# Feed-forward stage of a two-layer graph network: DVE operands moved from SBUF into PSUM, and a third PSUM bank for the down products

## Chip, cores and metric

The kernel runs on one core of one Trainium2 chip. The metric is device time in microseconds (us) of one execution; lower is better. PE is the matrix engine, DVE the vector engine, ACT the scalar engine, POOL the engine that issues indirect DMAs here, SP the queue of plain DMAs.

## What is computed

There are 10,000 nodes with 512 features and 160,000 edges sorted by destination. Cut to what matters:

```python
h = maximum(layernorm(x), 0)                                 # layer 0
msg = (h @ rel_W[r] + rel_b[r])[src]                         # r: type of the edge, 4 types
agg = segment_sum(msg, dst) / maximum(deg, 1)
x1  = layer_norm(h + h @ self_W + self_b + agg) * ln1_w + ln1_b
f   = gelu(x1 @ W1 + b1) @ W2 + b2                           # 512 -> 1024 -> 512
x   = x + layer_norm(x1 + f) * ln2_w + ln2_b
h   = maximum(layernorm(x), 0)                               # layer 1: two rounds of
h   = relu(h @ W_self + mean_over_edges(h) @ W_neigh + b)    # this line, then
out = x + h                                                  # the residual
```

## The kernel before

All is fp32, in blocks of 128 nodes: a first block of 16 nodes (called "full" in the code, the remainder of 10,000), then blocks 0 to 77. The program has four stages, told apart in the trace by the lines that run: preparation (the products per edge type, L724, and lists of edges, to about 1230 us of the span), the **feed-forward stage** (about 1230 to 3030 us, the first `with` in `aligned`), and two aggregation stages that end at 6251.8 us. The change touches the feed-forward stage alone.

**One round of the feed-forward stage** (the loop at L1107) handles one block. Its steps stand in each engine's queue in the order of the code; no scheduler reorders them, and every engine works its queue in order.

- `gather` (L790) makes POOL issue the indirect DMAs of the *next* block: 5 `orow` tiles and 11 `row` tiles of 128x512, and on every 4th (16th) block one (two) `srow` tiles. They land in a ring of 28 SBUF tiles (`rows`), so POOL may run ahead until a slot is still in use.
- `hots` (L811) makes DVE compare the constant `lane` (0 to 127 along the row) with the local indices `loc` and so write one-hot matrices for the next block (L820, 128x896).
- `second` (L1035) takes the finished down products `po`: DVE adds the residual `rest` to each (L1042, result in SBUF) and takes statistics (L1013, L1014).
- `add` (L854) makes DVE add the 11 `row` tiles into the block's PSUM bank `pa` (L858), after `sums` (L831) let PE put the one-hot products of the `orow` and `srow` tiles there (L847). L1126 scales the sum and adds the node's own value `xs`, and statistics follow.
- `products` (L1086) is the PE work of the round, before the next block's sums: a part of a group's feed-forward, and `turn` (L958), the transposes of the block of the round before (L963).
- `finish` (L1017) makes the scale factors: square root on ACT (L1020), then two small DVE steps (L1022, L1023). `scaled` (L1047) applies the norms: ACT subtracts and scales (L1028), DVE multiplies by the weight and adds (L1067 and L1068 for the first norm, L1072 and L1073 for the second).

A group is four blocks, and its feed-forward is spread over the four rounds after the one of its successor's first block. By the block number b of the round they are called here **A** (b mod 4 = 1: half of the up products, L975, with Gelu on ACT, L977), **B** (b mod 4 = 2: the other half), **C** (b mod 4 = 3: down products d0 and d1, L986) and **D** (b mod 4 = 0: d2 and d3). The first D is in the round of block 8, the last in that of block 76: 18 of them. In C and D the order on PE is: first product, transposes, second product, sums of the next block. In the first rounds PE also has 24 products of a kind put off from the preparation (`residuals`, L921, `LATE` says how many a round; each ends in a DVE addition, L928).

**PSUM** has eight banks of 128x512 fp32 here: `psA` 2 (`pa`), `psT2` 2 (transposes), `psH` 2 (up products), `psO` 2 (down products and `residuals`). A bank is taken again when the last reader of what it held is done.

Of the kernel before, what the change touches and what calls it, by code (L numbers as in the profile page):

```python
# [8 lines left out]
F32 = mybir.dt.float32  # L9
# [4 lines left out]
OP = mybir.AluOpType  # L14
# [7 lines left out]
def kernel(  # L22
# [739 lines left out]
    def aligned(ctxa):  # L762
# [27 lines left out]
        def gather(b, table, pool, split):  # L790

            def rows(n, idx, name=None, bufs=None):
                t = pool.tile([P, D], F32, name=name, bufs=bufs) if name else row_tile()
                nc.gpsimd.indirect_dma_start(  # L794
                    out=t[:n], out_offset=None, in_=table,
                    in_offset=bass.IndirectOffsetOnAxis(ap=idx, axis=0))
# [12 lines left out]
            return others, [rows(P, row[:, b, t:t + 1]) for t in range(own(b))]  # L809

        def hots(b, pool, scalar=False):  # L811
            n = OT + NL if b < full else OT_LAST
            hot = pool.tile([P, OT + NL, P], F32, name="hot", bufs=2)
            if scalar:
                for t in range(n):
                    nc.scalar.activation(hot[:, t, :], lane, AF.Abs, bias=loc[:, b, t:t + 1],  # L816
                                         scale=-1.0)
                nc.scalar.activation(hot[:, :n], hot[:, :n], AF.Relu, bias=ones[:, :1], scale=-1.0)
                return hot
            nc.vector.tensor_tensor(hot[:, :n].bitcast(F32R),  # L820
                                    lane[:, None, :].to_broadcast([P, n, P]),
                                    loc[:, b, :n].unsqueeze(2).to_broadcast([P, n, P]),
                                    op=OP.is_equal)
            return hot
# [3 lines left out]
            for _ in range(n):  # L828
                nc.tensor.matmul(p, ident, w, start=True, stop=True)  # L829

        def sums(b, others, hot, idle=None):  # L831

            r, n = height(b), len(others)
            pa = psA.tile([P, D], F32, name="pa")
# [15 lines left out]
        def begin(b, hot, table, pool, idle=None, split=False):  # L850
            others, mine = gather(b, table, pool, split)
            return sums(b, others, hot, idle), mine

        def add(b, pa, mine):  # L854

# [5 lines left out]
        with ExitStack() as s:  # L861
# [1 line left out]
            wp = s.enter_context(tc.tile_pool(name="wp2", bufs=1))  # L863
            gp = s.enter_context(tc.tile_pool(name="gp", bufs=1))
            sp = s.enter_context(tc.tile_pool(name="sp", bufs=3))
            psT = s.enter_context(tc.tile_pool(name="psT2", bufs=2, space=PSUM))
            psH = s.enter_context(tc.tile_pool(name="psH", bufs=2, space=PSUM))
            psO = s.enter_context(tc.tile_pool(name="psO", bufs=2, space=PSUM))
            w1s = wp.tile([P, KC, F], F32, name="w1s")
            w2s = wp.tile([P, FC, D], F32, name="w2s")  # L870
            b1s = wp.tile([P, FC], F32, name="b1s")
# [60 lines left out]
            fetch(LATE[0])  # L932
            for b in blocks[:2]:
                load(b)
            first_hot = hots(blocks[0], gp)
# [63 lines left out]
            class Scales:  # L999
# [27 lines left out]
                def apply(self, out, v, c, r, func):  # L1027
                    nc.scalar.activation(out, v, func, bias=self.rs[:r, 1, c:c + 1],  # L1028
                                         scale=self.rs[:r, 0, c:c + 1])

            rests = {}
            fed, third = [], []
            now = Scales()

            def second():  # L1035

                nonlocal fed
                got = []
                for b, po in fed:
                    r = height(b)  # L1040
                    v = rests.pop(b)
                    nc.vector.tensor_tensor(v[:r], po[:r], v[:r], op=OP.add)  # L1042
                    got.append((b, v, now.stats(v[:r], r)))
                fed = []
                return got

            def scaled(got, first):  # L1047

                nonlocal third, now
                if first:  # L1050
                    b, c = first
                    r, v = height(b), nodes[b]
                    now.apply(v[:r], v[:r], c, r, AF.Identity)
                if third:
                    h1, at = pair(h1_d, third[0][0], len(third), "h1", 2)
                    for k, (b, c) in enumerate(third):
                        now.apply(h1[:, k, :], xrs.pop(b), c, height(b), AF.Relu)
                    nc.sync.dma_start(at, h1)
                third = []
                for b, v, c in got:  # L1060
                    r = height(b)
                    now.apply(v[:r], v[:r], c, r, AF.Identity)
                if first:
                    b, c = first
                    r, v = height(b), nodes[b]
                    rests[b] = gp.tile([P, D], F32, name="rest", bufs=11)
                    nc.vector.tensor_tensor(rests[b][:r], v[:r], ln1w[:r], op=OP.mult)  # L1067
                    nc.vector.tensor_tensor(rests[b][:r], rests[b][:r], lnb2[:r], op=OP.add)  # L1068
                now = Scales()
                for b, v, c in got:  # L1070
                    r = height(b)
                    nc.vector.tensor_tensor(v[:r], v[:r], ln2w[:r], op=OP.mult)  # L1072
                    nc.vector.tensor_tensor(xrs[b], xrs[b], v[:r], op=OP.add)  # L1073
                    third.append((b, now.stats(xrs[b], r)))
                if got:
                    b, n = got[0][0], len(got)
                    nc.sync.dma_start(rows_of(xn_d, (b, n, height(b))), xrs.pop((b, n)))
# [5 lines left out]
            held = begin(blocks[0], first_hot, table, gp, split=True)  # L1083
            nc.vector.tensor_tensor(lnb2, lnb2, b2s, op=OP.add)

            def products(work, turned):  # L1086
# [20 lines left out]
            for bs in plan:  # L1107
                for b in bs:
                    r = height(b)
                    if b == bs[0]:  # L1110
                        before, grp = grp, Group(bs)
                    if i + 2 < len(blocks):
                        load(blocks[i + 2])
                    if i + 1 < len(blocks):
                        hot = hots(blocks[i + 1], gp)
                    ready = []
                    if i + 2 < len(LATE):
                        fetch(LATE[i + 2])
# [7 lines left out]
                    nc.vector.scalar_tensor_tensor(v[:r], pa[:r], rdeg[:r, b:b + 1], v[:r],  # L1126
                                                   op0=OP.mult, op1=OP.add)
                    first = (b, now.stats(v[:r], r))
                    part = products(queue.pop(0) if queue else [], turning)
                    next(part)  # L1130
                    now.finish()
                    scaled(got, first)
                    next(part, None)
                    if i + 1 < len(blocks):
                        held = begin(blocks[i + 1], hot, table, gp, split=True)
# [411 lines left out]
```

## Time and profile before

| | us |
|---|---|
| runs: median of 3 (lowest to highest) | 6250.86 (6247.69 to 6256.69) |
| the profiled execution: its own time | 6253.56 |
| the profiled execution: span of its instructions | 6251.8 |
| feed-forward stage: window 1400 to 2900, PE busy | 1427.8 of 1500 |
| the same, POOL busy | 1148.7 of 1500 |
| the same, DVE busy | 1127.8 of 1500 |

The page groups instructions by line, engine, operands and shape, with busy time and the mean of one in ns. The timeline gives start and length of single instructions (a row with "xN" merges N in a row), with the idle time before them in brackets and what ended it. A window view sums the busy time of each engine between two times, with the clock that PE was granted (1.00 is full speed). The page counts no instruction that only issues or waits, so POOL's rows are the issues of its gathers. In PE's rows a 128x512 product over 128 rows is two matmul instructions.

### The profile page before, as it was taken

Reading aid. Unit: us, or ns where it says so; the run is one execution under the profiler, and the core shown is the slowest. Engines: PE = TensorE matmul, PEld = TensorE weight load, DVE = VectorE, ACT = ScalarE, POOL = GpSimd, SP = SyncE. Lnnn points to the kernel's source line nnn. Section 1 sums busy time; section 2 is a strip of 40 time slices with the busy share of each in tenths; the row PEclk is TensorE's granted clock in tenths of the full one; section 3 lists DMA queues with packets and bytes.
Section 4 is the critical chain, followed back from the end, with each engine's and each line's share of the span. In section 5 each row is a group of like instructions: output and inputs, shape, how many; then the busy total and the mean of one; then the engine's idle time right before and its main releaser. Section 6 shows DMA issues by size and latency. Waiting matters only on the chain.

```text
span 6251.8 us, 54551 instructions
## 1 busy us (share of the span) xinstructions
PE 5699.4 (91%) x14875; PEld 2517.3 (40%) x14875; DVE 3597.1 (58%) x7253; ACT 1858.2 (30%) x3672; POOL 3762.9 (60%) x3927
## 2 busy tenths in 40 slices
PE   9999999989999999999788888888879888888888
PEld 3444444444444444444333333333333333333333
DVE  8768889557777777776344444344334444444444
ACT  1016565013333333333322222222222222222221
POOL 0001110057777777775477777777767777777776
PEclk9999999989999999999899999999999999999999
DMA  4333344387887878886577777777778788878877
GB/s 162 114 117 118 122 136 154 132 275 243 255 256 242 256 246 252 256 257 196 187 234 237 237 234 237 237 234 237 237 232 251 249 247 251 250 246 251 250 246 217
DMA packets 503498, 1373.74 MB, mean 220 GB/s; under 512 B 82206, under 2 KB 82206, under 8 KB 503054
## 3 DMA queue, kind: packets, MB, share of 16 engines
q0 software_dynamic: 308768, 1008.91, 54.0%
q1 hardware_dynamic: 193886, 360.20, 15.9%
q8 instruction: 120, 1.97, 0.1%
q14 instruction: 196, 1.61, 0.1%
q10 hardware_dynamic: 528, 1.05, 0.1%
HBM read 1156.54 MB, written 213.30 MB: 219 GB/s over the span
## 4 chain that ended last, share of the span: by engine, by line
DMA 40%; PE 39%; DVE 8%; issue 7%; POOL 5%; ACT 1%; POOLq 0%; SPq 0%; DVEq 0%; ACTq 0%
DMA rows<-h_d,row 19%; PE pm L724 15%; DMA rows<-h_d,orow 14%; PE pa L847 6%; POOL rows L794 5%; PE ph L975 5%; PE po L986 4%; DVE pa L858 4%; DMA rows<-hall_d,row 4%; PE pm L664 3%; PE po L1218 1%; PE po L926 1%; DVE st L1013 1%; PE pT L172 1%; DMA tail<-h_d,srow 1%
## 5 line engine op out<-in xcount | busy, mean ns | idle before, releaser
L858 DVE TENSOR_TENSOR pa<-pa,rows 128x512 f32<-128x512 f32 x2574 | 1799.3, 699 | 2061.3 <-PE pa L847 1241.3
L794 POOL DMA_INDIRECT rows<-h_d,row x1716 | 1622.2, 945 | 522.7 <-issue 291.2
L847 PE MATMUL pa<-rows,hot 128*128 128x512 f32 (+1 forms) x2358 | 1247.7, 644 | 371.4 <-DMA rows<-h_d,orow 314.2
L794 POOL DMA_INDIRECT rows<-hall_d,row x858 | 868.1, 1012 | 273.6 <-issue 109.0
L794 POOL DMA_INDIRECT rows<-h_d,orow x786 | 743.1, 945 | 354.4 <-DMA h_d<-h 99.0
L847 PEld LDWEIGHTS pa<-rows,hot 128*128 128x128 f32 (+1 forms) x2358 | 407.1, 194 | 1151.9 <-DMA rows<-h_d,orow 829.0
L794 POOL DMA_INDIRECT rows<-hall_d,orow x393 | 378.2, 962 | 346.0 <-DVE hg L666 202.2
L986 PE MATMUL po<-w2s,hid 128*128 128x512 f32 (+1 forms) x1264 | 566.6, 602 | 17.2 <-DVE rest L1042 14.0
L1218 PE MATMUL po<-wss,hTb 128*128 128x512 f32 (+1 forms) x1264 | 579.7, 602 | 0.0
L1189 PE MATMUL po<-wns,mTb 128*128 128x512 f32 (+1 forms) x1264 | 573.5, 597 | 1.4 <-ACT mTb L173 1.4
L975 PE MATMUL ph<-x1T,w1s 128*128 128x512 f32 (+2 forms) x1344 | 558.7, 568 | 4.8 <-ACT hid L977 4.8
L173 ACT COPY mTb<-pT 128x512 f32<-128x512 f32 (+1 forms) x158 | 91.8, 581 | 1233.5 <-PE pT L172 1233.5
L1214 ACT ACTIVATE mb<-pa,rdeg 128x512 f32<-128x512 f32 (+1 forms) x158 | 108.5, 687 | 1130.0 <-DVE pa L858 1127.8
L829 PE MATMUL pa<-wss,ident 128*128 128x512 f32 x936 | 427.5, 593 | 0.0
L508 POOL DMA_INDIRECT win<-rec_d,at x79 | 76.0, 962 | 545.9 <-PE pe L533 364.8
L1189 PEld LDWEIGHTS po<-wns,mTb 128*128 128x128 f32 (+1 forms) x1264 | 240.2, 190 | 308.4 <-issue 272.4
L975 PEld LDWEIGHTS ph<-x1T,w1s 128*128 128x128 f32 x1344 | 249.4, 192 | 282.0 <-issue 273.4
L986 PEld LDWEIGHTS po<-w2s,hid 128*128 128x128 f32 (+1 forms) x1264 | 237.6, 191 | 308.2 <-issue 283.4
L847 PE MATMUL pa<-tail,hot 128*128 128x512 f32 x624 | 308.1, 611 | 50.6 <-DMA tail<-h_d,srow 47.1
L816 ACT ACTIVATE hot<-lane,loc 128x128 f32<-128x128 f32 x1098 | 337.7, 391 | 0.0
L1218 PEld LDWEIGHTS po<-wss,hTb 128*128 128x128 f32 (+1 forms) x1264 | 233.5, 195 | 235.3 <-issue 234.9
L724 PE MATMUL pm<-wrel,hT 128*128 128x512 f32 x624 | 296.5, 597 | 0.0
(289 smaller groups left out, 6224.5 us busy)
## 6 DMA issues: line engine op xcount, KB each, us to landing
hall_d<-p SPq DMA_DIRECT2D x156, 256.0 KB, 2.5
hall_d<-u SPq DMA_DIRECT2D x156, 256.0 KB, 2.4
hb<-h_d SPq DMA_DIRECT2D x156, 256.0 KB, 4.3
rows<-h_d,row POOLq DMA_INDIRECT x1716, 3.8
xg<-in_x_dram SPq DMA_DIRECT2D x39, 512.0 KB, 3.6
xr_d<-xg SPq DMA_DIRECT2D x39, 512.0 KB, 3.0
xs<-xs_d SPq DMA_DIRECT2D x39, 512.0 KB, 7.6
h_d<-h SPq DMA_DIRECT2D x39, 512.0 KB, 4.5
```

Of the source, the lines that this page charges most:

```text
L664: nc.tensor.matmul(pm[:r], rows[3][:, c, k, :r], wself[:, k, :], start=(k == 0), stop=(k == KC - 1))
L724: nc.tensor.matmul(pm, a[:, k, :], w[:, k, :], start=(k == 0), stop=(k == KH - 1))
L794: nc.gpsimd.indirect_dma_start(out=t[:n], out_offset=None, in_=table, in_offset=bass.IndirectOffsetOnAxis(ap=idx, axis=0))
L816: nc.scalar.activation(hot[:, t, :], lane, AF.Abs, bias=loc[:, b, t:t + 1], scale=-1.0)
L829: nc.tensor.matmul(p, ident, w, start=True, stop=True)
L847: nc.tensor.matmul(pa[:r], h, v, start=(i == 0), stop=(i == len(work) - 1))
L858: nc.vector.tensor_tensor(pa[:r], pa[:r], t[:r], op=OP.add)
L975: nc.tensor.matmul(ph[:, :n], w1s[:, k, f * P:(f + 1) * P], self.xT[:, k, :n], start=(k == 0), stop=(k == KC - 1))
L986: nc.tensor.matmul(po[:r], self.hid[:, f, c * r:(c + 1) * r], w2s[:, f, :], start=(f == 0), stop=(f == FC - 1))
L1189: nc.tensor.matmul(po[:r], mT[:, k, :r], wns[:, k, :], start=False, stop=(k == KC - 1))
L1214: nc.scalar.activation(m[:r], pa[:r], AF.Copy, scale=rdeg[:r, b:b + 1])
L1218: nc.tensor.matmul(po[:r], hT[:, k, :r], wss[:, k, :], start=(k == 0), stop=False)
```

## The change

- `hots` no longer reads `lane` in SBUF: ACT copies it into the first 128 columns of the PSUM bank that the next block's sums will use (the bank is now taken there, `bank()`), and DVE compares from PSUM. `sums` gets the bank handed in.
- L1126's result stays in `pa` (PSUM); statistics and ACT's normalisation read it there, and ACT writes the normalised rows to `xs` in SBUF for the transposes. `second` leaves its sum in `po`.
- `affine` takes the place of L1067/L1068 and, with ACT's L1028 on `rest`, of L1072/L1073: two DVE steps, (v - mean) * weight in place in PSUM, then * scale + addend (`lnb2`, or the residual `xr`) into SBUF.
- In `scaled` the second norm's steps (`got`) now come before the first norm's (`first`).
- `psO` has three banks, `psT2` one.

```diff
-        def hots(b, pool, scalar=False):
+        def hots(b, pool, scalar=False, pa=None):
...
+            nc.scalar.copy(pa[:, :P], lane)
             nc.vector.tensor_tensor(hot[:, :n].bitcast(F32R),
-                                    lane[:, None, :].to_broadcast([P, n, P]),
+                                    pa[:, None, :P].to_broadcast([P, n, P]),
                                     loc[:, b, :n].unsqueeze(2).to_broadcast([P, n, P]),
                                     op=OP.is_equal)
...
-            psT = s.enter_context(tc.tile_pool(name="psT2", bufs=2, space=PSUM))
+            psT = s.enter_context(tc.tile_pool(name="psT2", bufs=1, space=PSUM))
             psH = s.enter_context(tc.tile_pool(name="psH", bufs=2, space=PSUM))
-            psO = s.enter_context(tc.tile_pool(name="psO", bufs=2, space=PSUM))
+            psO = s.enter_context(tc.tile_pool(name="psO", bufs=3, space=PSUM))
...
+                def affine(self, out, v, c, r, w, to):
+
+                    nc.vector.scalar_tensor_tensor(v, v, self.mv[:r, c, 0:1], w[:r],
+                                                   op0=OP.subtract, op1=OP.mult)
+                    nc.vector.scalar_tensor_tensor(out, v, self.rs[:r, 0, c:c + 1], to,
+                                                   op0=OP.mult, op1=OP.add)
...
-                    v = rests.pop(b)
-                    nc.vector.tensor_tensor(v[:r], po[:r], v[:r], op=OP.add)
-                    got.append((b, v, now.stats(v[:r], r)))
+                    nc.vector.tensor_tensor(po[:r], po[:r], rests.pop(b)[:r], op=OP.add)
+                    got.append((b, po, now.stats(po[:r], r)))
...
-                    now.apply(v[:r], v[:r], c, r, AF.Identity)
+                    now.apply(nodes[b][:r], pa[:r], c, r, AF.Identity)
...
-                for b, v, c in got:
+                last, now = now, Scales()
+                for b, po, c in got:
                     r = height(b)
-                    now.apply(v[:r], v[:r], c, r, AF.Identity)
+                    last.affine(xrs[b], po[:r], c, r, ln2w, xrs[b])
+                    third.append((b, now.stats(xrs[b], r)))
                 if first:
...
-                    nc.vector.tensor_tensor(rests[b][:r], v[:r], ln1w[:r], op=OP.mult)
-                    nc.vector.tensor_tensor(rests[b][:r], rests[b][:r], lnb2[:r], op=OP.add)
-                now = Scales()
-                for b, v, c in got:
-                    r = height(b)
-                    nc.vector.tensor_tensor(v[:r], v[:r], ln2w[:r], op=OP.mult)
-                    nc.vector.tensor_tensor(xrs[b], xrs[b], v[:r], op=OP.add)
-                    third.append((b, now.stats(xrs[b], r)))
+                    last.affine(rests[b][:r], pa[:r], c, r, ln1w, lnb2[:r])
...
                     if i + 1 < len(blocks):
-                        hot = hots(blocks[i + 1], gp)
+                        next_bank = bank()
+                        hot = hots(blocks[i + 1], gp, pa=next_bank)
...
-                    nc.vector.scalar_tensor_tensor(v[:r], pa[:r], rdeg[:r, b:b + 1], v[:r],
+                    nc.vector.scalar_tensor_tensor(pa[:r], pa[:r], rdeg[:r, b:b + 1], v[:r],
                                                    op0=OP.mult, op1=OP.add)
-                    first = (b, now.stats(v[:r], r))
+                    first = (b, now.stats(pa[:r], r), pa)
```

More of the change, by code (lines that the diff above doesn't have):

```diff
@@ L829, in keep_busy, with bank, sums @@
                 nc.tensor.matmul(p, ident, w, start=True, stop=True)
-        def sums(b, others, hot, idle=None):
+        def bank():
+            return psA.tile([P, D], F32, name="pa")
+        def sums(b, others, hot, idle=None, pa=None):
             r, n = height(b), len(others)
-            pa = psA.tile([P, D], F32, name="pa")
+            pa = pa or bank()
             if idle:
@@ L848, in sums, with begin @@
             return pa
-        def begin(b, hot, table, pool, idle=None, split=False):
-            others, mine = gather(b, table, pool, split)
-            return sums(b, others, hot, idle), mine
+        def begin(b, hot, table, pool, idle=None, pa=None):
+            others, mine = gather(b, table, pool, pa is not None)
+            return sums(b, others, hot, idle, pa), mine
         def add(b, pa, mine):
@@ L934, in aligned @@
                 load(b)
-            first_hot = hots(blocks[0], gp)
+            first_bank = bank()
+            first_hot = hots(blocks[0], gp, pa=first_bank)
             residuals(LATE[0])
@@ L1050, in scaled @@
                 if first:
-                    b, c = first
-                    r, v = height(b), nodes[b]
-                    now.apply(v[:r], v[:r], c, r, AF.Identity)
+                    b, c, pa = first
+                    r = height(b)
+                    now.apply(nodes[b][:r], pa[:r], c, r, AF.Identity)
                 if third:
@@ L1059, in scaled @@
                 third = []
-                for b, v, c in got:
+                last, now = now, Scales()
+                for b, po, c in got:
                     r = height(b)
-                    now.apply(v[:r], v[:r], c, r, AF.Identity)
+                    last.affine(xrs[b], po[:r], c, r, ln2w, xrs[b])
+                    third.append((b, now.stats(xrs[b], r)))
                 if first:
-                    b, c = first
-                    r, v = height(b), nodes[b]
+                    b, c, pa = first
+                    r = height(b)
                     rests[b] = gp.tile([P, D], F32, name="rest", bufs=11)
-                    nc.vector.tensor_tensor(rests[b][:r], v[:r], ln1w[:r], op=OP.mult)
-                    nc.vector.tensor_tensor(rests[b][:r], rests[b][:r], lnb2[:r], op=OP.add)
-                now = Scales()
-                for b, v, c in got:
-                    r = height(b)
-                    nc.vector.tensor_tensor(v[:r], v[:r], ln2w[:r], op=OP.mult)
-                    nc.vector.tensor_tensor(xrs[b], xrs[b], v[:r], op=OP.add)
-                    third.append((b, now.stats(xrs[b], r)))
+                    last.affine(rests[b][:r], pa[:r], c, r, ln1w, lnb2[:r])
                 if got:
@@ L1082, in aligned @@
             turning = None
-            held = begin(blocks[0], first_hot, table, gp, split=True)
+            held = begin(blocks[0], first_hot, table, gp, pa=first_bank)
             nc.vector.tensor_tensor(lnb2, lnb2, b2s, op=OP.add)
@@ L1134, in aligned @@
                     if i + 1 < len(blocks):
-                        held = begin(blocks[i + 1], hot, table, gp, split=True)
+                        held = begin(blocks[i + 1], hot, table, gp, pa=next_bank)
                     if b == bs[0] and before:
```

## The prediction

> **What bounds the kernel now.** First the page's groups, for who is dear in this stage:
>
> ```profile
> L794 POOL DMA_INDIRECT rows<-h_d,row x1716 | 1622.2, 945 | 522.7 <-issue 291.2
> ...
> L794 POOL DMA_INDIRECT rows<-hall_d,row x858 | 868.1, 1012 | 273.6 <-issue 109.0
> ```
>
> The same gather issue takes 945 ns in the aggregation stages (`h_d`) and 1012 ns here (`hall_d`). Next, POOL's groups for 1383 to 2927 us alone:
>
> ```profile
> L794 POOL DMA_INDIRECT rows<-hall_d,row x802 | 814.5, 1016 | 247.4 <-issue 100.2 <-DMA rows<-hall_d,row 46.6 <-DMA rows<-hall_d,orow 25.3
> L794 POOL DMA_INDIRECT rows<-hall_d,orow x360 | 344.9, 958 | 109.7 <-DVE pa L858 34.1 <-issue 28.0 <-DMA rows<-hall_d,row 25.9
> L794 POOL DMA_INDIRECT rows<-hall_d,srow x22 | 20.8, 944 | 6.8 <-issue 3.8 <-DMA rows<-hall_d,row 1.8 <-PE po L986 0.9
> ```
>
> Busy and idle sum to 1544.1 us, the whole window, and the idle is 0.307 us a gather, the step that POOL always makes between two. So POOL never waits: it is the bound. 1184 gathers at 0.945 would be 1118.9 busy instead of 1180.2: 61.3 us are lost. The timelines of POOL, then DVE, show where:
>
> ```profile
> 2240.10 0.94 POOL L794 DMA_INDIRECT rows<-hall_d,row  x1 [0.31 <-DMA rows<-hall_d,row]
> 2241.35 1.42 POOL L794 DMA_INDIRECT rows<-hall_d,row  x1 [0.30 <-DMA rows<-hall_d,row]
> 2243.07 1.61 POOL L794 DMA_INDIRECT rows<-hall_d,row  x1 [0.30 <-issue]
> ```
>
> ```profile
> 2241.26 0.69 DVE L1073 TENSOR_TENSOR wself<-wself,rest 128x512 f32<-128x512 f32 x1
> ...
> 2242.81 1.06 DVE L820 TENSOR_TENSOR hot<-lane,loc 128x896 fp32r<-128x896 f32 x1
> ...
> 2246.86 8.02 DVE L858 TENSOR_TENSOR pa<-pa,rows 128x512 f32<-128x512 f32 x11
> ```
>
> The long gathers lie beside DVE steps with two SBUF operands; beside L858, with one in PSUM, they keep 0.95. A page of the Trainium skill, "SBUF — State Buffer", section "Who interferes with whom", says otherwise: a `tensor_tensor` with two SBUF inputs blocks GpSimd's reads only, and descriptor issue is inferred to go free. By it POOL would keep its 84.9 us a group (below); the rows above, 1.42 and 1.61 for 0.95, decide for a gain.
>
> PE comes second. Where POOL is still ahead (rounds 6 to 15), PE's timeline is gapless, 19.39 us a round:
>
> ```profile
> 1527.62 7.03 PE L986 MATMUL po<-w2s,hid 128*128 128x512 f32 x16
> ...
> 1546.99 7.03 PE L986 MATMUL po<-w2s,hid 128*128 128x512 f32 x16
> 1553.86 0.60 PE L963 MATMUL pT<-ident,xs 128*128 128x128 f32 x4
> 1554.30 7.03 PE L986 MATMUL po<-w2s,hid 128*128 128x512 f32 x16
> ...
> 1566.39 7.03 PE L975 MATMUL ph<-x1T,w1s 128*128 128x512 f32 x16
> ```
>
> So a group costs POOL 65.25 gathers (4 x 16, 1 srow, 0.25 srow) x 1.301 = 84.9 us, and PE 4 x 19.39 = 77.6.
>
> **The change, part by part.**
>
> POOL: with every frequent two-SBUF step gone (the halves, L784 and L786, stay, once a group), a gather falls to 0.945 + 0.304: 81.5 us a group. If POOL stayed the bound this would be worth the 61 us.
>
> PE gets a new wait in round D. Three `psO` banks serve four products a group, so d3 takes the bank of d0. Before, d0's bank was free after L1042, at the start of DVE's round. Now it is free after `affine` on d0, at its end; in the changed kernel's order d3 waits for exactly that DVE step. Behind d3 in PE's queue stand the sums of block b+1, and behind those DVE's additions. Its length, with t = 0 at the end of C's issue of sums (1527.62 above) and PE gapless:
>
> - d3's turn without the wait: 1554.30 - 1527.62 = 26.7.
> - C's additions: start 0.2, 11 steps 8.05, to 8.3.
> - To D's additions: 11.2 in the trace (1537.45 to 1548.64: L1126, statistics, table load and root, scales, ACT, L1067, L1068, halves, hot, two L1042 with statistics). New in it: the hot comparison waits for ACT's copy of `lane`, which stands behind the halves' cast (+0.3), and two steps are scalar_tensor_tensor (0.75 as L1126, not 0.69: +0.1). 11.6, to 19.9; the sums of D end at 19.4, no bound.
> - D's additions 8.05, to 27.9. Then, from these rows, 1556.67 to 1559.19 for L1126, statistics, root and scales: 2.5, to 30.4:
>
> ```profile
> 1548.64 8.02 DVE L858 TENSOR_TENSOR pa<-pa,rows 128x512 f32<-128x512 f32 x11
> 1556.70 0.75 DVE L1126 SCALAR_TENSOR_TENSOR xs<-pa,rdeg,xs 128x512 f32<-128x512 f32 x1
> ...
> 1559.03 0.16 DVE L1023 SCALAR_TENSOR_TENSOR rs<-mv,rs 128x3 f32<-128x3 f32 x1
> ```
>
> - Two `affine` steps 1.6, and 0.1 to PE: d3 starts at 32.1 to 32.2. PE stands still for 5.5 us.
>
> The order of `got` before `first` shortens this; the other order would add 1.5. ACT's apply on `rest` leaves the loop, but DVE's in-place step on `pa` still waits for ACT's read, as L1067 did.
>
> Unknown: DVE steps with PSUM on both sides, and statistics from PSUM. About 12 of them are in this chain. Nearest rows: L1042 (0.67), L858 (0.70), L1126 (0.75); the far end is ACT's 0.81 for the same size. I take the rows of like operation; the ends move the stall to 5.1 (12 x 0.03 less) and 6.8 (12 x 0.11 more). The copy of `lane` (128x128) lies between ACT's 128x64 copy (0.21) and its 128x128 activation (0.45): 0.3.
>
> The clock adds to it. After a short stretch with PE mostly idle the next 3.41 us run at half speed (windows; PE busy is the first sum, the clock is PEclk):
>
> ```profile
> 2219.93:2223.34 3.41, 0.86 (x3) 0.45 (x4) 3.34 (x6) 1.06 (x3) 2.80 (x3) 1.00 0.68 186
> 2223.34:2226.75 3.41, 3.41 (x5) 1.35 (x6) 3.27 (x7) 0.00 (x0) 2.50 (x4) 0.50 0.65 196
> ```
>
> The product there took 8.83 for 7.03. In the trace windows with over about 1.75 of 3.41 idle are followed by half speed. A 5.5 us gap always holds one; by its place in the grid it costs 0.8 to 2.6 us, on average 1.6. The skill's page "TensorE: Matmul & The Clock Gate", "What's actually happening", asks for a whole idle window; a gap of 5.5 holds one in 61% of places, so by the rule about 0.8 a gap and 14 us less in the sum. The rows with 0.86 busy speak for the dearer one.
>
> So D costs 5.5 + 1.6 = 7.1, a group 77.6 + 7.1 = 84.7: more than POOL's new 81.5, nearly POOL's old 84.9. **PE and DVE take POOL's place as the bound.** POOL then runs ahead until the ring stops it; the slot reused is 28 gathers back, freed some 15 us or more before its row is needed, so the ring hurts nobody.
>
> Sum, from block 8's transposes (1476.32) to round 77's (2926.64), 1450.3 us before: 69 rounds x 19.39 = 1337.9, 18 D x 7.1 = 127.8, together 1465.7: **+15.4**. POOL was ahead here at first, so before was cheaper than 84.9 a group.
>
> Start: with three banks two waits go. At 1301.2 PE waits 3.2 us for L928, then runs a half-speed window (8.83 for 7.03); at 1369.8 it waits 3.1 for L928 and takes 8.74. PE is late there (DVE waits for its sums), so both count: 4.6 + 4.8 = **-9.4**. The like wait at 1397.8 stays: the third bank is then held by the first block's product until `affine`. Nothing is late in place of these; rows landed earlier.
>
> Tail after 2927: without ACT's apply on `rest` (1.5 for two), waits for ACT shrink at 2934 (1.1), 2939 (0.7), 2990 (1.5) and at the end (0.9): **-4.2**. d3 there waits for no addition: `affine` ends about 5.5 after d1, d2 takes 6.9.
>
> `psT2` with one bank: the last transposes were read 18 us earlier; free. The preparation and aggregation stages have the same instructions.
>
> 15.4 - 9.4 - 4.2 = +1.8 on the profiled execution's 6253.6 (span 6251.8): 6255. The median of the runs shown, 6250.9, is 2.7 lower, so 6255 stands 4 above it.
>
> **Rivals.** A measurement here tells about 0.2% (12.5 us) from no change.
>
> *Faster: d3's wait is covered and POOL stays the bound.* For it: the 61 us are real, and PE has 81.5 - 77.6 = 3.9 us a group to spare. Against: 7.1 is more than 3.9. If all is covered, 6253.6 - 61 - 4 = 6189; if the half-speed windows fail to come and the stall is at its low end, 18 x (1.6 + 0.4) = 36 less, 6219.
>
> *Slower: the copy of `lane` holds DVE up.* In B it stands on ACT behind the last Gelu, which follows root, two applies and a table load (1.28). By my count hot is ready just as PE's sums end, with no reserve. Each us over that delays C's additions and so d3, 18 us in all; it decides from 0.7 us. At 2 us (one more table load and Gelu, 1.28 + 0.69): 6291.
>
> *POOL's loss is not DVE's doing and stays.* Then 84.9 beside 84.7 a group, ends that don't always meet: 6262 to 6275.
>
> **Chances.** Forecast's case 0.50, faster 0.20, slower 0.25, no relief 0.05. The forecast's own range is 6239 to 6291 (18 D at 6.2 to 9.1: stall 5.1 to 6.8, clock 1.1 to 2.3), mostly within the bound: 0.40 same, 0.05 each side. With 0.18, 0.22 and 0.04 of the rivals outside it: faster 0.23, same 0.46 (0.40 and 0.02, 0.03, 0.01 of the rivals), slower 0.31. The range of 8 in 10 is 6222 to 6294.
>
> **What would show it.** Right: gathers at 0.95; POOL idle now, waiting for slots; PE idle about 5.5 us before each d3, ended by `affine` (L1040 after), then half speed; groups of 84 to 85 us with rounds A to C at 19.4. Wrong: gathers above 1.0, no wait at d3, or DVE's hot waiting for ACT by more than 1 us in B.

## The result, and the profile after

The kernel after takes 6262.1 us (median of 16 runs, 6259.3 to 6265.7), the kernel before beside it 6253.2 (16 runs, 6247.6 to 6257.9). The ratio is 1.0016, 95% interval 1.0008 to 1.0023: 9 to 10 us slower, which the forecast counted as no change, and 7 us above the forecast time. The profiled execution of after has a span of 6259.6 us, 7.8 more than before's 6251.8.

Of the experiments, `second_norm_sbuf` and `sums_before_d3_4` ran on chips where the kernel before takes 6253 and 6265 us (called undisturbed here); all others fell on chips where it takes about 7100 because engines stand still there for some 10 us at a time (disturbed; last section), and of those the whole times are not read as prices, only the rows between the halts.

The groups of the page of after (busy us, mean ns of one, idle us before them and what ended most of it), first the gathers of the aggregation, then those of the feed-forward stage, then the down products:

```profile
L794 POOL DMA_INDIRECT rows<-h_d,row x1716 | 1622.1, 945 | 522.7 <-issue 285.7
...
L794 POOL DMA_INDIRECT rows<-hall_d,row x858 | 812.3, 947 | 316.7 <-issue 118.8
...
L991 PE MATMUL po<-w2s,hid 128*128 128x512 f32 (+1 forms) x1264 | 605.5, 636 | 85.8 <-DVE wself L1040 57.3
```

The stage's gathers now cost what those of the aggregation cost, 947 ns for 1012. The relief is there. The third line shows who took the place: the down products have 85.8 us of idle time ahead of them, most of it ended by L1040, the second step of `affine`. The waits between 1400 and 2900 us (who waited for whom, us in total, times, longest) say the same, and that POOL now has time to spare, waiting for the sums to free its slots:

```profile
DVE pa L862 <- PE pa L851: 83.4, 49, 3.6
POOL rows L794 <- PE pa L851: 69.0, 76, 4.3
PE po L991 <- DVE wself L1040: 52.5, 11, 4.9
DVE hot L821 <- ACT pa L820: 47.8, 53, 2.0
...
PE po L991 <- DVE xr L1040: 28.6, 6, 4.8
```

The two rows with L1040 are 17 waits and 81.1 us, 4.77 each: one in each round D of the window. PE's timeline of one round D (start, length, and in brackets the idle time before and what ended it), with d2, the transposes, d3 and the next group's first up products:

```profile
2223.40 7.03 PE L991 MATMUL po<-w2s,hid 128*128 128x512 f32 x16
2230.26 0.60 PE L968 MATMUL pT<-ident,xs 128*128 128x128 f32 x4
2235.62 9.89 PE L991 MATMUL po<-w2s,hid 128*128 128x512 f32 x16 [4.76 <-DVE wself L1040]
```

DVE's timeline of the same round, from the additions to the step that frees d0's bank:

```profile
2223.60 8.03 DVE L862 TENSOR_TENSOR pa<-pa,rows 128x512 f32<-128x512 f32 x11 [1.07 <-PE pa L851]
...
2234.03 0.75 DVE L1038 SCALAR_TENSOR_TENSOR po<-po,mv,ln2w 128x512 f32<-128x512 f32 x1
2234.81 0.75 DVE L1040 SCALAR_TENSOR_TENSOR wself<-po,rs,wself 128x512 f32<-128x512 f32 x1
```

L1040 ends at 2235.56, d3 starts at 2235.62. And d3 takes 9.89 us where d2 took 7.03. The windows of 3.41 us around the gap (length, then busy time of PE, PE's weight loads, DVE, ACT and POOL, the granted clock, DMA share, GB/s) show why:

```profile
2227.59:2231.01 3.42, 3.27 (x11) 1.45 (x9) 3.25 (x6) 0.00 (x0) 2.59 (x3) 1.00 0.72 200
2231.01:2234.42 3.41, 0.00 (x0) 0.00 (x0) 2.91 (x7) 0.52 (x2) 2.72 (x3) 1.00 0.74 225
2234.42:2237.83 3.41, 2.21 (x3) 1.17 (x4) 3.27 (x6) 1.94 (x5) 2.50 (x4) 0.50 0.73 211
2237.83:2241.25 3.42, 3.42 (x5) 1.35 (x4) 2.98 (x6) 0.88 (x2) 2.51 (x4) 0.50 0.76 229
2241.25:2244.66 3.41, 3.41 (x9) 1.50 (x8) 1.98 (x4) 0.67 (x1) 1.74 (x2) 1.00 0.99 326
```

One window without any PE work, then two at half clock. d3 lies in the slow stretch from 2235.62 to 2241.25, 5.63 us, and loses half of it, 2.8.

Rounds A, B and C last 19.37 to 19.40 each in after, from transposes to transposes, rounds D 27.1 to 27.2 (the first 26.80, the second 26.98). So **where the time went**, by the transposes of rounds 8 and 77 and the end of the stage:

| | before | after | difference | forecast |
|---|---|---|---|---|
| to round 8 | 1476.3 | 1463.0 | -13.3 | -9.4 |
| round 8 to round 77 | 1450.3 | 1477.1 | +26.8 | +15.4 |
| round 77 to the stage's last step | 97.0 | 91.5 | -5.5 | -4.2 |
| the aggregation stages | 3228.2 | 3228.0 | -0.2 | 0 |
| sum | | | +7.8 | +1.8 |

### The profile page after: what moved, and what is told of

Same layout as the page of the kernel before. It is cut to its first block, busy times and chain, and to the rows that moved or that the text cites. A ratio compares the mean times of both kernels' runs of the same rounds, so it can differ in the third digit from the quotient of the medians.

```text
span 6259.6 us, 54531 instructions
## 1 busy us (share of the span) xinstructions
PE 5695.6 (91%) x14875; PEld 2528.2 (40%) x14875; DVE 3625.4 (58%) x7253; ACT 1816.8 (29%) x3672; POOL 3700.4 (59%) x3927
## 4 chain that ended last, share of the span: by engine, by line
DMA 34%; PE 8%; issue 6%; POOL 5%; DVE 2%; ACT 0%; POOLq 0%; SPq 0%; DVEq 0%; ACTq 0%
DMA rows<-h_d,row 20%; DMA rows<-h_d,orow 13%; POOL rows L794 4%; PE pa L851 3%; DVE pa L862 1%; PE po L1225 1%; PE po L991 1%; PE ph L980 1%; PE po L1196 1%; DMA tail<-h_d,srow 1%; PE pa L830 0%; PE pT L172 0%; DMA rows<-hall_d,row 0%; DMA hb<-h_d 0%; POOLq L794 0%
## 5 line engine op out<-in xcount | busy, mean ns | idle before, releaser
L851 PE MATMUL pa<-rows,hot 128*128 128x512 f32 (+1 forms) x2358 | 1223.4, 634 | 336.2 <-DMA rows<-h_d,orow 322.6
L794 POOL DMA_INDIRECT rows<-hall_d,row x858 | 812.3, 947 | 316.7 <-issue 118.8
L991 PE MATMUL po<-w2s,hid 128*128 128x512 f32 (+1 forms) x1264 | 605.5, 636 | 85.8 <-DVE wself L1040 57.3
L830 PE MATMUL pa<-wss,ident 128*128 128x512 f32 x936 | 427.6, 593 | 0.0
L991 PEld LDWEIGHTS po<-w2s,hid 128*128 128x128 f32 (+1 forms) x1264 | 254.6, 204 | 398.5 <-issue 306.4
```

The lines of the kernel that those rows point to most:

```text
L794: nc.gpsimd.indirect_dma_start(out=t[:n], out_offset=None, in_=table, in_offset=bass.IndirectOffsetOnAxis(ap=idx, axis=0))
L991: nc.tensor.matmul(po[:r], self.hid[:, f, c * r:(c + 1) * r], w2s[:, f, :], start=(f == 0), stop=(f == FC - 1))
```

## The experiments

**Theory.** The change does relieve POOL of some 60 us, but d3 of every round D must now wait for `affine`, and the clock makes d3 slow besides: 4.8 + 2.8 us, 18 times. PE takes POOL's place as the bound at nearly the same period. **Rivals.** The period is DVE's or the ring's, and PE's gap only shows the slack; d3 is slow for a reason other than the clock; POOL's relief is worth nothing in itself.

**1. The sums ahead of d3** (`sums_before_d3`, one kernel measured four times). In rounds D the next block's sums are put in the gap:

```diff
+                    early = b < full and b % 4 == 0 and b >= 8
+                    if early:
+                        held = begin(blocks[i + 1], hot, table, gp, pa=next_bank)
                     next(part, None)
-                    if i + 1 < len(blocks):
+                    if i + 1 < len(blocks) and not early:
                         held = begin(blocks[i + 1], hot, table, gp, pa=next_bank)
```

> The kernel after, with one change: in each of the 18 rounds D, PE gets the sums of the next block ahead of the transposes and d3, not behind d3. Theory 1 (what keeps the 61 us of POOL from being collected is d3's wait for affine, 4.8 us, and the half speed after it, 2.9): the sums take 5.9 us of the gap, d3's turn comes at 32.6 of the round pair where its bank is free at 31.4, so PE has no gap before d3 and no slow product; PE then has 77.6 us a group, POOL is the bound again, now at 65.25 x 1.25 = 81.5, gapless from 1383 on: 1184 gathers end some 61 us earlier than before, the tail is 5 shorter, about 6187 us, 6180 to 6200. Rival 2 (DVE's chain or the ring sets the period of 85.3 and PE's gap is only where the slack shows): the gap moves to another place and the time stays within 8 us of 6262. Rival 3 (the 5.9 us are not enough, part of the wait stays): between the two, with a wait on L1040 of 1 us or more left in the trace.

The first measurement and the next two:

> The same kernel as sums_before_d3, on another turn of the chip, since in the first one (the kernel before took 7107 us there) ACT and PE stood still for 10 us and more at a time while nothing that they wait for was late, in all stages that gather, and a term of 7.7 us a D round can't be told from that. Where before takes about 6250 again: theory 1 (d3's wait and the half speed behind it are what keeps POOL's 61 us from being collected) 6180 to 6200; rival 2 (the period of 85.3 is set elsewhere) 6254 to 6270; rival 3 (part of the wait stays) between, with a wait on L1040 of 1 us or more left.

> The same kernel as sums_before_d3, now that before takes 6253 again. Theory 1 (d3's wait and the half speed behind it keep POOL's 61 us from being collected): no wait on L1040 ahead of d3, d3 in 7.03, POOL gapless from about 1383 on at 1.25 us a gather, 6187, 6180 to 6200. Rival 2 (the period of 85.3 is set elsewhere): 6254 to 6270. Rival 3 (part of the wait stays): between.

were on the disturbed chips: 7154.6 against 7107.3 for before (ratio 1.0066, interval 1.0041 to 1.0091), 7168.4 against 7110.7 (1.0083, 1.0050 to 1.0116) and 7159.9 against 7100.1 (1.0090, 1.0058 to 1.0122). There the order is a loss, and none of the three expectations held. The fourth measurement was on an undisturbed chip:

> The same kernel as sums_before_d3. The two other turns fell on chips where before takes 7100 and engines stand still once a group without a visible reason. Where before takes 6253: theory 1 (d3's wait and the half speed behind it keep POOL's 61 us from being collected): no wait on L1040 ahead of d3, d3 in 7.03, POOL the bound at 81.5 us a group, 6187, 6180 to 6200, which is 28 below second_norm_sbuf (6215), where 21 of the 61 us stay lost. Rival 2 (the gathers hold DVE's additions back as soon as POOL is the bound, and with them affine and d3: the wait comes back in its new place): 6205 to 6240, with d3 still waiting for L1040 by 1 us and more.

Measured: 6199.0 against 6265.0 for before, ratio 0.9896, interval 0.9879 to 0.9912, or 66 us less; theory 1's 6187 against 6253 was 66 less too. PE's timeline of a round D (d2, the sums of the next block with a short wait for their rows, the transposes, d3, the next group's first up products):

```profile
2264.92 7.03 PE L991 MATMUL po<-w2s,hid 128*128 128x512 f32 x16
...
2276.45 7.37 PE L851 MATMUL pa<-rows,hot 128*128 128x512 f32 x10 [3.58 <-DMA rows<-hall_d,orow]
2283.66 0.60 PE L968 MATMUL pT<-ident,xs 128*128 128x128 f32 x4
2284.09 7.03 PE L991 MATMUL po<-w2s,hid 128*128 128x512 f32 x16
2290.96 7.03 PE L980 MATMUL ph<-x1T,w1s 128*128 128x512 f32 x16
```

No wait at d3, and 7.03 for it. PE's gap has not vanished: it waits 3.58 us for rows ahead of the sums, and these then take 7.37 us at a granted clock of 0.60, where the same ten instructions take 4.45 at full speed. But PE now waits for POOL, whose groups between 1400 and 2850 show that it never rests (idle 0.306 and 0.305 a gather, the step it always makes):

```profile
L794 POOL DMA_INDIRECT rows<-hall_d,row x780 | 741.2, 950 | 238.5 <-issue 81.4 <-DMA rows<-hall_d,row 51.8 <-DMA rows<-hall_d,orow 21.0
L794 POOL DMA_INDIRECT rows<-hall_d,orow x354 | 335.5, 948 | 107.9 <-DVE pa L862 32.6 <-issue 28.0 <-DMA rows<-hall_d,row 27.1
```

Theory 1 stands: with d3's wait gone the whole of POOL's relief is collected, and POOL is the bound again at 0.95 + 0.31; the first rival, that DVE or the ring sets the period, falls. On the undisturbed chip this order beats before and, by the ratios to before (0.9896 and 1.0016), after as well; on the disturbed chips it loses to before.

**2. The second norm in SBUF again** (`second_norm_sbuf`): the sum in `second` goes to `rest`, ACT subtracts and scales there, two DVE steps with two SBUF operands follow, all as before; the first norm, the comparison and the banks stay as after.

```diff
-                    nc.vector.tensor_tensor(po[:r], po[:r], rests.pop(b)[:r], op=OP.add)
-                    got.append((b, po, now.stats(po[:r], r)))
+                    v = rests.pop(b)
+                    nc.vector.tensor_tensor(v[:r], po[:r], v[:r], op=OP.add)
+                    got.append((b, v, now.stats(v[:r], r)))
...
-                    last.affine(xrs[b], po[:r], c, r, ln2w, xrs[b])
+                    nc.vector.tensor_tensor(v[:r], v[:r], ln2w[:r], op=OP.mult)
+                    nc.vector.tensor_tensor(xrs[b], xrs[b], v[:r], op=OP.add)
```

> The kernel after, with the second norm alone as before: the sum of po and rest goes to SBUF, ACT subtracts and scales it there, DVE multiplies by the weight and adds the residual in two steps with two SBUF operands. d0's bank is then free at the start of D's DVE work, as before. Theory 1 (d3's wait and the clock behind it, 7.7 us a D round, are what the change pays; POOL's relief is real but not collected): no wait at d3, PE at 77.6 us a group, POOL the bound; its loss beside DVE is cut to what lies beside those 8 steps of 0.69 a group, 5.5 of the 15.2 us a group that had two SBUF operands before, so about 22 of the 61 us stay lost. On a chip where before takes 6250: 6253 - 39 - 3 (tail) = 6211, 6200 to 6225. Rival 2 (the relief itself is not worth anything, the period is set by DVE or DMA): 6245 to 6260. On a chip as slow as in the last two turns, where engines stand still without a visible reason, the same shows only in the rounds between these halts: no wait on L1040 ahead of d3, and d3 in 7.03.

Measured on an undisturbed chip: 6215.1 against 6253.4, ratio 0.9940, interval 0.9923 to 0.9956; 38 us less where 42 were expected. PE's waits between 1400 and 2850 no longer hold L1040; POOL's `row` gathers do not rest (0.305 a gather) and are a little longer:

```profile
PE pa L851 <- DMA rows<-hall_d,orow: 39.0, 30, 3.4
PE pa L851 <- DVE pa L1138: 3.6, 2, 2.4
PE pa L851 <- ACT upper L787: 2.1, 3, 0.9
PE ph L980 <- ACT hid L982: 0.6, 4, 0.2
```

```profile
L794 POOL DMA_INDIRECT rows<-hall_d,row x769 | 753.3, 980 | 234.5 <-issue 79.5 <-DMA rows<-hall_d,row 52.7 <-DMA rows<-hall_d,orow 30.5
```

Of the 26.9 us that its gathers take beyond 0.945 each, 25.2 lie beside the two steps put back. So relief in part, without d3's wait, beats relief in full with it: which operands go to PSUM matters less here than whose bank they hold.

**3. Products of no use in the gap** (`filled_gap`, one kernel measured three times). Five products go ahead of each d3 of a round D, into the bank that the next sums overwrite; nothing is left out of the computation.

```diff
+                    if fill and i == len(work) - 1:
+                        keep_busy(next_bank, ln1w, 5)
                     got.append(call())
```

> The kernel after, with five further products of 128x512 in front of each d3 of a round D (ident times ln1w, into the bank that the next block's sums then overwrite; no result depends on them). PE waits for affine as before, but is busy for 4.4 of the 4.8 us. Theory 1 (the 9.89 us that d3 takes for 7.03 are the clock's answer to the gap): d3 takes 7.0 to 7.1, 18 x 2.86 = 51 us less than after, about 6211, 6205 to 6220, with groups of 82.4 us where POOL needs 81.5. Rival 2 (d3 is slow for another reason, such as reading hid while ACT and DVE are at work, or the filling only moves the slow window): d3 stays near 9.9 and the time within 6 us of 6262. Rival 3 (only a gap that holds a whole window of 3.41 us counts, so part of the d3 were never slow): 18 x 1.75, about 6231.

> The same kernel as filled_gap, now that before takes 6253 again: five products of no use ahead of each d3 of a round D. Theory 1 (d3's 9.89 us for 7.03 are the clock's answer to the gap): the wait's length of 4.8 stays, filled but for some 0.4; d3 takes 7.0 to 7.1; 6262 - 18 x 2.86 = 6211, 6205 to 6220. Rival 2 (d3 is slow for another reason): d3 near 9.9 and 6256 to 6268. Rival 3 (only a gap that holds a whole window of 3.41 us counts): about 6231.

> The same kernel as filled_gap (five products of no use ahead of each d3 of a round D), for a chip where before takes 6250 to 6265. Relative to before, after stood at +10 us. Theory 1 (d3's 9.89 us for 7.03 are the clock's answer to the gap): d3 takes 7.0 to 7.1, 18 x 2.86 = 51 us less than after, so 41 us below before (ratio 0.993 to 0.995), with D rounds of 24.3 in place of 27.2 and groups of 82.4. Rival 2 (d3 is slow for another reason): D rounds of 27.2, ratio 1.000 to 1.003. Rival 3 (only a gap that holds a whole window of 3.41 us counts): 21 us below before, ratio 0.996 to 0.998. Rival 4 (with the gap filled POOL, which needs 81.5 a group, is so near that the two take turns as the bound): rounds D of 24.3, but others above 19.4, 25 to 40 us below before.

All three measurements fell on a disturbed chip: ratios to before 1.0004 (0.9984 to 1.0025), 1.0011 (0.9987 to 1.0035) and 1.0011 (0.9993 to 1.0029), and not the 0.993 to 0.995 of theory 1. What the filling is worth in time was therefore not shown; the shortest rounds D of the three traces last 24.8 us, where after has 27.17 and theory 1 had 24.3. But each of the three traces has 18 products d3 with a gap left ahead of them that differs with the halts, and so tells what the clock does. Two of them, from the second and the first trace (L830 is the filling):

```profile
2304.43 4.46 PE L830 MATMUL pa<-ln1w,ident 128*128 128x512 f32 x10
2310.39 7.13 PE L991 MATMUL po<-w2s,hid 128*128 128x512 f32 x16 [1.50 <-issue]
```

```profile
2103.57 4.46 PE L830 MATMUL pa<-ln1w,ident 128*128 128x512 f32 x10
2111.49 8.83 PE L991 MATMUL po<-w2s,hid 128*128 128x512 f32 x16 [3.46 <-issue]
```

PE stood idle or filling for 5.8 and 7.8 us between transposes and d3, longer than the 4.8 of after, and the first d3 is not slow. Over the 54: with 0.8 to 1.7 us of true idle time left, 15 of 15 took 7.13; with 1.8 to 3.2, 4 of 17 took 7.1 and 13 some 8.8 (one slow window, 1.7 lost); with 3.4 us and more, all 22 took 8.6 to 10.2 but one, which lies in four pieces with halts between them. With the filling in it, a gap of 5.8 us is followed by a d3 of 7.13. So d3's length follows PE's idle time, not its wait: the clock's part of theory 1 stands, rival 2 falls. Rival 3, that only a gap with a whole window in it counts, falls as well: 13 gaps of 1.9 to 3.0 us were followed by half speed, and they cannot hold 3.41.

**4. The first norm first again** (`first_norm_first`): in `scaled` the block `if first` goes back ahead of the loop over `got`.

```diff
+                if first:
+                    ...
+                    last.affine(rests[b][:r], pa[:r], c, r, ln1w, lnb2[:r])
                 for b, po, c in got:
                     ...
                     last.affine(xrs[b], po[:r], c, r, ln2w, xrs[b])
-                if first:
-                    ...
-                    last.affine(rests[b][:r], pa[:r], c, r, ln1w, lnb2[:r])
```

> The kernel after, with the order within scaled put back: the first norm's affine (on pa) ahead of the second norm's (on po). It puts 1.50 us of DVE (0.75 + 0.75) in front of the step that frees d3's bank. Theory 1 (the time in the stage hangs on that wait): the wait grows from 4.8 to 6.3, 18 x 1.5 = 27 us, half speed a few tenths more or less a round: about 6289, 6283 to 6300. Rival 2 (the period is set elsewhere): within 5 us of 6262.

On a disturbed chip: 7167.4 against 7107.3, ratio 1.0089 (1.0063 to 1.0115), and 61 us above `filled_gap` on the same chip. The shortest gap ahead of d3 is this one:

```profile
2533.53 9.34 PE L991 MATMUL po<-w2s,hid 128*128 128x512 f32 x16 [7.25 <-issue]
```

From transposes to d3 it is 2.1 us more than the shortest in `filled_gap` on that chip (5.1, filling included), where 1.5 us of DVE were put in front. That agrees with theory 1, by which the wait grows with what stands ahead of `affine`; on a chip with halts one pair of shortest gaps doesn't show it, and the size in time cannot be had there.

**5. Two banks again** (`two_banks`): `psO` 2 and `psT2` 2 in after.

> The kernel after with the banks put back: two for the down products, two for the transposes. d2 then takes d0's bank, which is free only after affine on d0 in the same round. Theory 1: PE stands still ahead of d2, from the end of D's sums (19.7 of the round pair) to 32.2, 12.5 us in place of 4.8, with half speed behind it as now; 18 x 7.7 = 139 us, and the 13 us gained at the start go back: about 6414, 6395 to 6440. Rival 2 (the third bank is of no weight for the time in the middle of the stage, since all of it waits on DVE's chain anyway): 6262 + 13 = 6275.

On a disturbed chip: 7254.9 against 7107.3, ratio 1.0206 (1.0170 to 1.0242). PE stands still ahead of d2, in the least disturbed rounds for 12.1 to 13.2 us, where 12.5 was expected:

```profile
2477.75 8.78 PE L991 MATMUL po<-w2s,hid 128*128 128x512 f32 x16 [12.06 <-issue]
2486.36 0.60 PE L968 MATMUL pT<-ident,xs 128*128 128x128 f32 x4
2486.80 7.03 PE L991 MATMUL po<-w2s,hid 128*128 128x512 f32 x16
```

Results kept in PSUM with two banks make PE wait out 12 us of a round D's DVE chain; the third bank hides all of it but the 4.8 us.

**6. The third bank alone** (`before_three_banks`): `psO` 3 and `psT2` 1 in before.

> The kernel before, with three banks for the down products and one for the transposes, and nothing else. In the kernel after PE gets to block 8 13.3 us earlier (9.4 was forecast for the two waits on L928 that go). Theory 1: what comes behind is bound by POOL, which has no idle time after 1383 and waits for a slot only ahead of that; only what moves POOL's last wait for a slot counts, so not 13.3 but 3 to 8 us: about 6248. Rival 2 (a start gain is a gain whatever comes behind): 6253 - 13 = 6240. Rival 3 (nothing of it is left): 6253.

On a disturbed chip: 7102.5 against 7100.1, ratio on record 0.9992 (0.9966 to 1.0018). This tells none of the three apart. Only the mechanism shows: at 1301 PE goes on without the 3.2 us for L928.

```profile
1300.77 0.42 PE L963 MATMUL pT<-ident,xs 16*128 16x16 f32 x4
1301.11 7.13 PE L926 MATMUL po<-wself,rows 128*128 128x512 f32 x16
```

**7. The comparison alone** (`before_hot_psum`): in before, ACT copies `lane` to the next bank and DVE compares from there; all else as before.

> The kernel before, with the one-hot comparison alone changed: ACT copies lane into the next block's PSUM bank, DVE compares from there. In the trace of before, of the 61.4 us by which gathers take longer than 0.945 between 1383 and 2927, 29.4 lie beside this comparison, 9.2 beside L1067/L1068 and 21.1 beside L1072/L1073. Theory 1 (POOL is the bound, what DVE's second SBUF operand costs it is the whole price): 29 us are gained, about 6224, 6218 to 6230. Rival 2 (a gather is held up by any DVE step, so the loss moves to the next one): 6245 to 6255. Rival 3 (the copy on ACT, behind Gelu, holds DVE back by its 2.0 us in some rounds and that counts): 6235 and more.

On a disturbed chip: 7084.5 against 7100.1, ratio on record 0.9996 (0.9969 to 1.0022); no price can be read, and what the comparison alone is worth in time stays open. The gathers can be read: between 1400 and 3100 us theirs take 27.4 us beyond 0.945 each, some 25 of it beside the norms' four steps with two SBUF operands and none beside the comparison (no gather there takes over 0.96 us), while in `before_three_banks`, on the same chip, some 27 of 59.4 lie beside it. The loss doesn't move to the next step: rival 2 falls.

## Why the prediction was right, and where its steps were off

The forecast's mechanism holds: POOL is relieved, d3's wait for `affine` and half speed behind it take the gain back, and PE and DVE are the bound. That its time came within 7 us (6255 against 6262) is partly luck. Over 18 rounds D the wait was put some 13 us too long and the clock's part some 22 too short, each outside the ends that the forecast itself gave it (5.1 to 6.8 and 1.1 to 2.3 us), and start and tail gained 5 us more than was put.

- **POOL's relief: right.** 0.945 us a gather was forecast, 0.947 measured. The inference that descriptor issue goes free of a `tensor_tensor` with two SBUF inputs (the Trainium skill, "SBUF — State Buffer", "Who interferes with whom") does not hold for these gathers: each such step taken away or put back takes its part of the long gathers with it (none beside the comparison in 7, 25.2 us beside the two steps put back in 2). A gather also reads its row numbers from SBUF, and reads are what the section does say is blocked; which part of the issue is held up, no run tells. A small slip in the sum: 1544.1 us for 1184 gathers is 1.304 each and 85.1 a group, not 1.301 and 84.9.
- **The new wait: right place, 4.8 for 5.5.** By the forecast's clock (t = 0 at 2204.01) the additions start at 19.6, not 19.9, and L1040 ends at 31.55, not 32.0; and PE's idle time begins at the end of the transposes, 26.85, where the forecast counted from d3's turn, 26.7. The chain up to the additions was no longer the bound: it ended 1.07 us before PE's sums. What was mis-sized is the table load in C. It was counted between statistics and root; in after it comes right behind ACT's copy, 10 us ahead of the root, and its 1.28 us are off the chain:

```profile
2202.42 0.27 ACT L820 COPY pa<-lane 128x128 f32<-128x128 f32 x1
2202.71 1.28 ACT L1025 ACT_TABLE_LOAD   x1
2214.02 0.29 ACT L1025 ACTIVATE rs<-mv,eps 128x1 f32<-128x1 f32 x1 [10.03 <-DVE mv L1019]
```

- **The clock: 2.8 for 1.6**, the term that was most off. The forecast used one threshold both ways, about 1.75 us idle in a window, and averaged over the places of the gap in the windows. But the first slow window, with 1.2 us idle, did not bring full speed back: by the forecast's rule d3 would have lost 1.1 us there, and it lost another 1.7 in the second. And the place is not random (last section). The Trainium skill's page "TensorE: Matmul & The Clock Gate", "What's actually happening", which was weighed against it, says that the clock comes back after a window of sustained work: the window at half clock with 2.21 us of work did not bring it back and the one with 3.42 did, which agrees. Its other half, that a whole idle window is needed, does not agree with the 13 slow d3 behind gaps of 1.9 to 3.0 us in experiment 3.
- **D in sum: 7.7 for 7.1**, 18 times: +26.8 in the middle of the stage for +15.4.
- **The start: -13.3 for -9.4.** The two waits on L928 went as said (with what they cost by the forecast's own rows, 3.2 + 1.8 and 3.1 + 1.7, it would have been -9.8). What was missed is that before runs at half clock twice more there: from 1326 to 1347 and from 1347 to 1368 its granted clock was 0.92 and 0.84, in after 1.00. The same product of 8 instructions, before and after:

```profile
1350.87 6.40 PE L926 MATMUL po<-wself,rows 128*128 128x512 f32 x8
```

```profile
1345.05 3.68 PE L930 MATMUL po<-wself,rows 128*128 128x512 f32 x8
```

The window ahead of each slow stretch is without idle time on record (3.42 of 3.42 us busy), much of it products with only 16 columns; why the clock fell there in before and not in after is open.
- **The tail: -5.5 for -4.2.** Fewer waits on ACT, as said.
- **The rival "slower" has its mechanism and no price.** Behind the last Gelu of a round B the comparison does wait 2.03 us for ACT's copy, three times the point from which the forecast let it count, and more than the 1 us that it had named as a sign of being wrong. That sign misled. PE's sums end later still (DVE then waits another 0.39 for them), and rounds B and C last 19.39: the wait stays inside the time that DVE has. The step "no reserve" was wrong: there are these 0.39 us, and another 1.07 ahead of D's additions (shown above), so by an estimate from these rows some 1.5 us more would have been needed to make d3 later:

```profile
2202.72 1.09 DVE L821 TENSOR_TENSOR hot<-pa,loc 128x896 fp32r<-128x896 f32 x1 [2.03 <-ACT pa L820]
2204.20 8.04 DVE L862 TENSOR_TENSOR pa<-pa,rows 128x512 f32<-128x512 f32 x11 [0.39 <-PE pa L851]
```

- **The rival "faster"** was the right account of what the wait keeps back: with d3's wait covered the time is 66 us below before (experiment 1), as that rival had it (65).

What stays open: the time of `filled_gap`, `first_norm_first`, `two_banks`, `before_three_banks` and `before_hot_psum` on an undisturbed chip.

## What to carry to other kernels

A result left in a PSUM bank moves the bank's release from the first reader to the last, and with a fixed number of banks that makes a wait of everything in between; look for the product that takes the bank next and for what can be put in front of it. Where an engine that is relieved was the bound by a few us a group, the second engine's new wait decides, and moving work that is ready into the gap (here the next block's sums) collects what the change only made possible. An idle PE costs its gap and the slow windows behind it (4.8 and 2.8 us here); price both.

## What the runs showed of the hardware

**The group locked to the clock's windows.** d3 took 9.52, 9.70, 9.71, 9.81, 9.86, 9.88, 9.88, 9.90 us in the first eight rounds D of after and 9.89 to 9.92 from then on, and the slow stretches of the granted clock begin 85.33 us apart (2149.09, 2234.42, 2319.75), which is 25 windows of 3.413. The later d3 starts within the slow stretch, the less it loses, by half of the shift, so a group that comes late catches up: this is an explanation from the numbers, not tried. If it holds, a wait shorter by a few tenths would have bought nothing here.

**Engines that stand still on some chips.** On the chips where before takes 7100 us a gather's issue is as long as elsewhere (946 and 945 ns in `filled_gap`), and the preparation (0 to 1200 us) shows the busy times of after, window by window. But in the stages with gathers an engine stays idle about once a group with nothing late that the profile shows. PE's transposes of one round of `filled_gap`, first trace, and ACT's steps behind them:

```profile
1974.98 0.60 PE L968 MATMUL pT<-ident,xs 128*128 128x128 f32 x4
```

```profile
1981.84 0.78 ACT L1033 ACTIVATE xs<-pa,rs 128x512 f32<-128x512 f32 x1 [0.49 <-issue]
1993.74 1.50 ACT L970 ACTIVATE x1T<-pT,ln1bc,ln1wc 128x128 f32<-128x128 f32 x4 [11.13 <-PE pa L851]
```

L970 reads the transposes, done at 1975.6, and the profile names sums that it does not read; in after the same step follows L1033 at once (2215.47 after 2214.80). Which round is hit depends on the kernel (mostly C in `filled_gap`, B in `sums_before_d3`), and the kernel that wins 66 us elsewhere loses 47 to 60 there. What causes the halts was not found.
